# Gated products turned by the load in squares of 32 and by VectorE within them, in a two-layer adaLN feed-forward kernel

## The chip, the cores and the metric

The kernel runs on one core of a Trainium2 chip. The metric is the device time of one execution in microseconds (us), as the median of several executions.

A core has engines that run side by side, each with its own queue of instructions: TensorE (PE, matrix products; "PEld" is its loading of weights), VectorE (DVE), ScalarE (ACT), GpSimd (POOL) and SyncE (SP, which here issues nearly all transfers). Results of PE land in PSUM, everything else lies in SBUF, both with 128 partitions.

## What is computed

```python
def _L0_ffn_ref(x, A, B, Wr):
    ...
    scores = xf @ Wr.T
    top_vals, top_idx = jax.lax.top_k(scores, TOPK)          # 16 of 64
    gates = jax.nn.softmax(top_vals, axis=-1)
    G = jnp.zeros((N, K), xf.dtype).at[jnp.arange(N)[:, None], top_idx].set(gates)
    h = jnp.einsum('nd,krd->nkr', xf, A)
    out = jnp.einsum('nkr,kdr->nd', h * G[:, :, None], B)
    return (out * SCALING).reshape(*prefix, -1)
...
x = x + _L0_ffn_ref(_L0_cond_ref(x, cond_512, ...), L0_ffn_A, L0_ffn_B, L0_ffn_Wr)
x = x + _L1_ffn_ref(_L1_cond_ref(x, cond_512, ...), L1_ffn_qweight, ..., L1_ffn_bias)
```

x is (32, 64, 1024) fp32. `_cond_ref` is a chain of four one-dimensional convolutions whose weights depend on the conditioning vector. The first feed-forward layer is a mixture of 64 experts of rank 16: 2048 rows of 1024 numbers are multiplied by A (1024 x 1024, with the router's 64 columns beside it), the products h are gated, and the gated h is multiplied by B (1024 x 1024). The second feed-forward layer is a linear map whose weights are unpacked from int4.

## The kernel before

**Tiles.** The 2048 rows are cut into 16 pairs p (two samples of 64 channels, 128 rows each). `NP` is 16, `NC` is 8 (blocks of 128 along 1024), `H` is 512, `L` is 1024.

**Products in three parts.** A product in fp32 is made of three products of split operands. An operand's upper part is cut out by DVE (`high`, line 149: two shifts), DVE or POOL subtract it from the operand to get the lower part (line 918 for activations on DVE, line 374 for weights on POOL), ACT copies the upper part (lines 922 and 375) and scales the lower part of activations (line 926), and a third operand is the difference of both (line 934 for activations on POOL, line 382 for weights on DVE). In names, `thh`, `tlh` and `tdh` are upper, lower and difference of a pair's h; `hh` is the cut before the copy; `wb0` to `wb7` are B's eight row blocks with all three parts, and `wbh` the cut of one half of a block. `product` (line 954) runs first the upper and lower parts into one PSUM bank (Q), for each half of the 1024 columns, and then the difference into another (D): 48 products of 128x512 for a pair. Pairs 0 and 1 (`WHOLE`) take undivided fp32 operands instead, 16 products.

**Stages.** The first conv chain and the product with A run pair by pair (`layer0`); the gated h of pair p is stored to memory (`hgd[p]`, line 1062). Then, from about 399 to 630 us, a loop over p (line 1411) makes the product with B (`layer0b`). For each p it emits, in this order: the turning of pair p+1's h (`turned_h`), the load of pair p+2's h (`load_h`), and the product of pair p with its joins. h has its rows on partitions and must have the 1024 contracted columns there, so `turned_h` makes eight 128x128 transposes on PE (line 1078) into two PSUM banks; for pairs 0 and 1 ACT copies each bank (line 1087), for the others the split reads the bank. A join adds the product to the residual: line 1122 for the D part, line 1123 for the Q part, both on DVE, reading PSUM. After that x1 is stored and differences of its columns, `dd`, are made and stored for the next conv chain (lines 1159 to 1174).

**B's splits.** B's eight row blocks are loaded as they are (`load_b`, line 410: five blocks beside pair 14 of `layer0`, three beside pair 15). Blocks 0 to 3 are split beside the raw product of pair 0, blocks 4 to 7 beside that of pair 1; pair 2 is the first to use all of them. Each block costs two cuts on DVE (128x512), two subtractions on POOL (128x512), two copies on ACT, and one crossing on DVE (128x1024, line 382).

**Order.** Every engine runs its queue in the order in which the program emits; the exceptions are written out (`issue_after`). Next-layer work lies between the last pairs: the ends of the conv chain (lines 465 to 586), and the first conv groups of the second layer (lines 755 to 773). Buffers come from rings: "w4" with three for hs, hg, x1 and others, "hi" with three for cuts, two for `th` and `tl`, one for `td`; PSUM has three banks "cps" for turned h and conv groups and four "fps" for the products o.

Of the kernel before, what the change touches and what calls it, by code (L numbers as in the profile page):

```python
# [8 lines left out]
F32 = mybir.dt.float32  # L9
I32 = mybir.dt.int32  # L10
# [5 lines left out]
P = 128  # L16
# [8 lines left out]
NC = L // P  # L25
H = 512
# [37 lines left out]
def adaln_ffn_kernel(ctx: ExitStack, tc: tile.TileContext, t, out: bass.AP):  # L64
    nc = tc.nc
# [4 lines left out]
    wk = ctx.enter_context(tc.tile_pool(name="wk", bufs=2))  # L70
# [8 lines left out]
    def cpst(name):  # L79
        return cps.tile([P, H], F32, tag="cps", name=name)  # L80
# [8 lines left out]
    ident = const.tile([P, P], F32, name="ident")  # L89
# [28 lines left out]
    hgd = dram.tile([NP, P, L], F32, name="hgd")  # L118
# [19 lines left out]
    def tokens(tag, name, dt=F32R):  # L138

        return tok.tile([P, NC, P], dt, tag=tag, name=name, bufs=1 if tag == "td" else 2)  # L140
# [5 lines left out]
    def high(src, name):  # L146

        v = wk.tile([P, H], I32, tag="hi", name=name, bufs=3)[:, : src.shape[1]]
        nc.vector.tensor_scalar(
            v, src.bitcast(I32), BITS, BITS, ALU.logical_shift_right, ALU.logical_shift_left  # L150
        )
        return v.bitcast(F32)
# [254 lines left out]
    def load_b(ks, into):  # L407
        for k in ks:
            r = cv[:, k * L : (k + 1) * L]
            nc.sync.dma_start(r, t["bm"][k * P : (k + 1) * P])  # L410
            into.append(r)

    def load_q():
# [500 lines left out]
    def split(ps, shape, hi, lo, name, hold=False):  # L914

        uppers[name] = high(ps, name)
        h = shape(uppers[name])
        done["lo"] = nc.vector.tensor_tensor(lo, shape(ps), h, ALU.subtract)
        if hold:
            held.append((hi, h))  # L920
        else:
            nc.scalar.copy(hi, h)

    def scaled_low(v):
        v = v.rearrange("p a b -> p (a b)")
        nc.scalar.activation(v, v, AF.Copy, scale=RADIX)  # L926

    toks = {}
# [133 lines left out]
        nc.sync.dma_start(hgd[p], hs[:, E:])  # L1062

    def load_h(p):
        hg = wk.tile([P, L], F32, tag="w4", name=f"hg{p}", bufs=3)
        nc.sync.dma_start(hg, hgd[p])
        return hg

    def turned_h(p, hg):
        whole = p in WHOLE  # L1070
        key = f"h{p}"
        th = tokens("th", f"th{key}", F32 if whole else F32R)
        toks[key] = [th] if whole else [th, tokens("tl", f"tl{key}")]
        for g in range(2):
            ps = cpst(f"ht{p}_{g}")
            for c in range(4):
                k = 4 * g + c
                nc.tensor.transpose(  # L1078
                    ps[:, c * P : (c + 1) * P], hg[:, k * P : (k + 1) * P], ident
                )  # L1080
            ks = slice(4 * g, 4 * g + 4)

            def d(v):
                return v[:, ks].rearrange("p a b -> p (a b)")

            if whole:
                nc.scalar.copy(d(th), ps)
            else:
                split(ps, lambda v: v, d(th), d(toks[key][1]), f"hh{p}_{g}")
        if not whole:  # L1090
            scaled_low(toks[key][1])

# [253 lines left out]
    for k in range(NP):  # L1346
# [5 lines left out]
        if last:  # L1352
            hg = load_h(0)
# [35 lines left out]
        if last:  # L1389
            load_b(range(5, NC), braw)  # L1390
            turned_h(0, hg)
        elif k + 1 in WHOLE:
            outer(k + 1)
# [3 lines left out]
        if k == NP - 2:  # L1397
            load_b(range(5), braw)
# [6 lines left out]
        if not last:  # L1405
            crossed(f"x0_{k + 1}")

    hg = load_h(1)
    set1 = factors(1, cv[:, : 3 * AW], cv[:, 3 * AW : O_Y + Y])
    qw = None  # L1410
    for p in range(NP):
        if p + 1 < NP:
            turned_h(p + 1, hg)
        if p + 2 < NP:
            hg = load_h(p + 2)
# [127 lines left out]
```

## Time and profile before

| | us |
|---|---|
| median of 4 runs | 897.26 (896.24 to 898.35) |
| the profiled execution | 897.98 |
| its span, first to last instruction | 895.9 |

What the page and the trace show of the stage around the change:

| group | count | ns, median | where |
|---|---|---|---|
| transposes of h, PE, line 1078 | 128 | 273 | 398.7 to 584.2 us |
| ACT copies of turned h, line 1087 | 4 | 602 | 399.5 to 400.9 |
| cut of h from PSUM, DVE, line 149 | 28 | 679 | 416.1 to 587.1 |
| subtraction of the cut, DVE, line 918 | 28 | 682 | 417.9 to 587.8 |
| difference, POOL, line 934 (one at 520.26) | | 2410 | |
| cut of B, DVE, line 149 | 16 | 782 | 386.4 to 433.8 |
| subtraction for B, POOL, line 374 | 16 | 1447 | 398.1 to 435.5 |
| crossing for B, DVE, line 382 | 8 | 2062 | 401.3 to 437.6 |
| load of h, SP queue, line 1066 | 16 | | 512 KB each |

A group's median is the time of one instruction, not what it adds: PE overlaps instructions, and a queue that waits for another engine shows the wait either as idle time before the instruction or, where the engine is held within it, as a longer instruction. The starts of two successive products on PE are the surest measure of a stage; from 519.85 to 531.64 us, one pair's transposes and 48 products take 11.79 us. First products of the pairs start at 400.63 (p=0), 415.24, 429.76, 446.08, 459.06 and 471.26 us (p=5).

### The profile page before, as it was taken

How to read it: one execution, taken by the hardware profiler on the slowest of the kernel's cores; microseconds unless marked ns; L12 is line 12 of the kernel's file. 1: busy time of each engine (PE TensorE's matmuls, PEld its weight loads, DVE VectorE, ACT ScalarE, POOL GpSimd, SP SyncE). 2: the span in 40 equal slices, each digit the busy share in tenths (PEclk: the TensorE clock that was granted, in tenths of full speed). 3: DMA queues.
4: the chain of work that ended last, by engine and by line, in shares of the span. 5: the costliest groups of instructions: out<-in, count | busy, mean ns of one | idle time of the engine just before them, and what ended most of it. 6: DMA issues, size and time to landing. Idle time of an engine off the chain costs nothing.

```text
span 895.9 us, 14914 instructions
## 1 busy us (share of the span) xinstructions
PE 865.6 (97%) x5033; PEld 775.2 (87%) x5033; DVE 721.8 (81%) x1458; ACT 352.6 (39%) x817; POOL 531.6 (59%) x747
## 2 busy tenths in 40 slices
PE   5989999999999999999999999999999999999997
PEld 4877888999999999994688888787899999999997
DVE  4474898888888888778986665669999999999996
ACT  6344443444444444333332221246333443343340
POOL 7234654666666666556572222343787888888884
PEclk9999999999999999999999999999999999999999
DMA  8521212223222221344365665555433325324321
GB/s 246 148 72 54 54 56 75 77 90 88 80 84 86 83 79 71 107 176 156 136 231 193 207 193 185 188 168 173 168 123 108 107 90 148 117 90 138 122 66 71
DMA packets 49739, 109.81 MB, mean 123 GB/s; under 512 B 13700, under 2 KB 22400, under 8 KB 49664
## 3 DMA queue, kind: packets, MB, share of 16 engines
q1 hardware_dynamic: 48704, 107.88, 38.4%
q10 hardware_dynamic: 960, 0.99, 0.4%
q8 instruction: 40, 0.66, 0.3%
q14 instruction: 35, 0.29, 0.1%
HBM read 70.97 MB, written 37.88 MB: 121 GB/s over the span
## 4 chain that ended last, share of the span: by engine, by line
PE 73%; DVE 15%; issue 4%; POOL 4%; ACT 2%; DMA 2%; ACTq 0%; DVEq 0%; SPq 0%; POOLq 0%
PE h L954 18%; PE o L954 16%; PE q L1203 11%; PE f L618 6%; PE r L874 5%; PE c L772 5%; PE r L833 3%; PE r L842 2%; PE g L595 2%; PE c L767 2%; DMA x1e<-dd 1%; DVE cv L715 1%; PE p L825 1%; PE ht L1078 1%; DVE rt L865 1%
## 5 line engine op out<-in xcount | busy, mean ns | idle before, releaser
L715 DVE TENSOR_TENSOR cv<-cv 128x257 f32<-128x257 f32 x120 | 105.1, 908 | 1.3 <-ACT cv L757 0.9
L729 POOL TENSOR_TENSOR cv<-cv 128x256 f32<-128x256 f32 x120 | 77.7, 647 | 29.4 <-DVE cv L715 16.0
L721 POOL TENSOR_TENSOR cv<-cv 128x128 f32<-128x128 f32 x100 | 39.0, 411 | 67.6 <-PE r L842 48.2
L1203 PE MATMUL q<-wq,thx 128*128 128x342 f32 x384 | 73.0, 332 | 2.6 <-ACT thx L912 2.1
L954 PE MATMUL h<-wa,tdx 128*128 128x352 f32 (+1 forms) x336 | 72.4, 351 | 0.2 <-DVE wa L382 0.2
L1203 PE MATMUL q<-wq,tlx 128*128 128x342 f32 x384 | 72.4, 330 | 0.0
L618 PE MATMUL f<-gs,iw 128*128 128x128 f32 (+1 forms) x384 | 68.8, 329 | 0.0
L618 PEld LDWEIGHTS f<-gs,iw 128*128 128x128 f32 x384 | 62.5, 192 | 5.8
L954 PE MATMUL h<-wa,thx 128*128 128x352 f32 (+1 forms) x336 | 64.7, 333 | 0.0
L1203 PEld LDWEIGHTS q<-wq,thx 128*128 128x128 f32 x384 | 60.3, 189 | 4.6 <-ACT thx L912 3.2
L769 ACT ACTIVATE yt<-c,be,al 128x257 f32<-128x257 f32 x56 | 31.7, 567 | 81.1 <-PE c L767 81.0
L874 PE MATMUL r<-cv 128*128 128x128 f32 x480 | 63.4, 274 | 0.0
L1203 PEld LDWEIGHTS q<-wq,tlx 128*128 128x128 f32 x384 | 61.9, 189 | 0.8
L954 PE MATMUL h<-wa,tlx 128*128 128x352 f32 (+1 forms) x336 | 62.4, 327 | 0.0
L954 PE MATMUL o<-wb,thh 128*128 128x512 f32 x224 | 59.9, 401 | 1.5 <-ACT wb L375 1.5
L934 POOL TENSOR_TENSOR tdx<-thx,tlx 128x1024 fp32r<-128x1024 f32 x14 | 34.7, 2478 | 44.4 <-ACT tlx L926 36.2
L1122 DVE SCALAR_TENSOR_TENSOR cv<-o,cv 128x512 f32<-128x512 f32 x26 | 18.0, 691 | 51.8 <-PE o L954 51.8
L954 PEld LDWEIGHTS h<-wa,tdx 128*128 128x128 f32 x336 | 57.1, 188 | 2.4 <-DVE wa L382 0.5
L954 PE MATMUL o<-wb,tlh 128*128 128x512 f32 x224 | 58.5, 398 | 0.0
L874 PEld LDWEIGHTS r<-cv 128*128 128x128 f32 x480 | 58.4, 191 | 0.0
L633 ACT COPY cv<-f 128x256 f32<-128x256 f32 x64 | 24.0, 375 | 85.3 <-PE f L618 45.8
L641 POOL TENSOR_TENSOR cv<-cv 128x256 f32<-128x256 f32 x60 | 48.9, 815 | 12.2 <-ACT cv L636 12.2
(312 smaller groups left out, 2273.5 us busy)
## 6 DMA issues: line engine op xcount, KB each, us to landing
cv<-in_x_dram SPq DMA_DIRECT2D x60, 256.0 KB
cv<-x1e SPq DMA_DIRECT2D x64, 192.5 KB
x1e<-dd SPq DMA_DIRECT2D x16, 514.0 KB
hgd<-hs SPq DMA_DIRECT2D x16, 512.0 KB
hg<-hgd SPq DMA_DIRECT2D x16, 512.0 KB
x1d<-x SPq DMA_DIRECT2D x16, 512.0 KB
xb<-x1d SPq DMA_DIRECT2D x16, 512.0 KB
out_dram<-o SPq DMA_DIRECT2D x15, 512.0 KB
```

Source lines behind the costliest of these rows:

```text
L618: done["f"] = nc.tensor.matmul(pv[:, n : n + 2 - k], iw[:, e].rearrange("p a b -> p (a b)"), v, start=(m == 0), stop=(m == len(steps) - 1) ...
L641: nc.gpsimd.tensor_tensor(f[:, 4 * P : 6 * P].rearrange("p (a b) -> p a b", b=P), v[:, :, 0], v[:, :, 1], ALU.add,)
L715: nc.vector.tensor_tensor(d[:, k], yo[:, k : k + HQ], yb, ALU.subtract)
L721: nc.gpsimd.tensor_tensor(y[:, YB + k * P : YB + (k + 1) * P], y[:, 2 * k : 2 * k + 2 * P - 1 : 2], y[:, 1 : 2 * P : 2], ALU.subtract,)
L729: nc.gpsimd.tensor_tensor(e[:, :, k], d[:, :, 2 * k : 2 * k + HQ - 2 : 2], d[:, :, 1 : HQ - 1 : 2], ALU.subtract,)
L769: nc.scalar.activation(yt, mid, AF.Identity, bias=be0[:, n : n + 1], scale=a)
L772: done["c"] = nc.tensor.matmul(ps, w[:, q], xe[:, o : o + w_], start=True, stop=True)
L833: nc.tensor.matmul(ps[:, (2 + j) * P : (3 + j) * P], d[:, j, 1 : HQ - 1 : 2], w(6 + j), start=True, stop=True,)
L874: done["r"] = nc.tensor.matmul(ps[:, j * P : (j + 1) * P], y[:, YE + (2 * q + k) * P : YE + (2 * q + k + 1) * P], w(q + 2 * k), start=True ...
L934: done["td"] = nc.gpsimd.tensor_tensor(*(v.rearrange("p a b -> p (a b)") for v in (td, *toks[key])), ALU.subtract)
L954: nc.tensor.matmul(banks[l == 2], toks[key][l][:, order(k)], w[:, cols], start=(k == first and l != 1), stop=(k == last and l in (2, min(n ...
L1203: nc.tensor.matmul(ps, half[:, k], wq[at(k)][:, c * QC : (c + 1) * QC], start=(k == 0 and j == 0), stop=(k == NC - 1 and j == 1),)
```

## The change

The 128 transposes on PE go. A 128x128 transpose is a transpose of a 4 by 4 grid of squares of 32, and of each square within. The grid is now turned by the load: `load_h` makes four transfers, each to 32 partitions, with pieces of 256 numbers; quarter b of h's columns goes to partitions 32b to 32b+31, and quarter a of the rows lies beside it along the free axis. The squares are turned by a VectorE transpose, which turns every square of 32 by 32 by itself, two instructions of 128x512 for each pair. With this, block c of the turned h has column 256 b + 32 c + i on partition 32 b + i, and not column 128 c + partition, so `load_b` brings B's rows in the same order, by four transfers of 32 rows for each block. For pairs 0 and 1 the VectorE transpose writes the product's operand itself, and the four ACT copies go. For the others it writes a new SBUF tile, `ht`, from the ring "hi", and the split reads that tile instead of a PSUM bank.

```diff
     def load_b(ks, into):
         for k in ks:
             r = cv[:, k * L : (k + 1) * L]
-            nc.sync.dma_start(r, t["bm"][k * P : (k + 1) * P])
+            rows_of_b = t["bm"].rearrange("(b c i) d -> b c i d", b=4, c=NC)
+            for b in range(4):
+                nc.sync.dma_start(r[32 * b : 32 * b + 32], rows_of_b[b, k])
             into.append(r)
...
     def load_h(p):
+
         hg = wk.tile([P, L], F32, tag="w4", name=f"hg{p}", bufs=3)
-        nc.sync.dma_start(hg, hgd[p])
+        src = hgd[p].rearrange("(a j) (b x) -> b j a x", a=4, b=4)
+        for b in range(4):
+            nc.sync.dma_start(hg[32 * b : 32 * b + 32].rearrange("j (a x) -> j a x", a=4), src[b])
         return hg
...
         for g in range(2):
-            ps = cpst(f"ht{p}_{g}")
-            for c in range(4):
-                k = 4 * g + c
-                nc.tensor.transpose(
-                    ps[:, c * P : (c + 1) * P], hg[:, k * P : (k + 1) * P], ident
-                )
             ks = slice(4 * g, 4 * g + 4)
...
             if whole:
-                nc.scalar.copy(d(th), ps)
+                v = d(th)
             else:
-                split(ps, lambda v: v, d(th), d(toks[key][1]), f"hh{p}_{g}")
+                v = wk.tile([P, H], I32, tag="hi", name=f"ht{p}_{g}", bufs=3).bitcast(F32)
+            nc.vector.transpose(
+                v.rearrange("p (c a j) -> p a c j", c=4, a=4),
+                hg.rearrange("p (a c i) -> p a c i", a=4, c=NC)[:, :, ks],
+            )
+            if not whole:
+                split(v, lambda v: v, d(th), d(toks[key][1]), f"hh{p}_{g}")
         if not whole:
             scaled_low(toks[key][1])
```

The emission order of `turned_h`, `load_h` and `layer0b` in the loop stays. In the program as it is built, though, operations can stand elsewhere in an engine's queue than before, since some are placed by when their operands come free: on DVE the transposes of pair 1 stand behind the crossing of wb3, those of pair 2 ahead of the cuts of wb4, the copy of line 311 ahead of the second cut of wb4; in the later pairs the joins of line 1123 stand behind the second subtraction of the next pair. On SP the load of pair p+2's h stands behind the stores of an earlier pair's x1, and loads of B and of the first pairs' h stand behind the stores of h of pairs 14 and 15.

## The prediction

> **What bounds the kernel now.** The totals by engine first: TensorE (PE) is busy for 97% of the span, and the chain that ended last lies 73% on PE and 15% on VectorE (DVE). Line 1078, the transposes that the change removes, is 1% of that chain.
>
> ```profile
> PE 865.6 (97%) x5033; PEld 775.2 (87%) x5033; DVE 721.8 (81%) x1458; ACT 352.6 (39%) x817; POOL 531.6 (59%) x747
> PE 73%; DVE 15%; issue 4%; POOL 4%; ACT 2%; DMA 2%; ACTq 0%; DVEq 0%; SPq 0%; POOLq 0%
> ```
>
> Shares are averages, so next the busy time in stretches of the only stage that is touched (about 380 to 590 us). Columns: stretch and its length, busy us (instructions) of PE, PEld, DVE, ACT, POOL, then granted clock, DMA share, GB/s.
>
> ```profile
> 517.00:529.00 12.00, 12.00 (x59) 10.01 (x58) 7.09 (x10) 2.72 (x5) 2.81 (x4) 1.00 0.65 205
> ...
> 400.00:420.00 20.00, 20.00 (x58) 9.54 (x57) 16.45 (x19) 5.89 (x13) 12.14 (x11) 1.00 0.35 131
> 420.00:440.00 20.00, 18.49 (x59) 11.18 (x58) 17.66 (x16) 9.11 (x21) 15.55 (x22) 0.91 0.43 131
> 440.00:460.00 20.00, 20.00 (x108) 17.16 (x107) 17.80 (x29) 7.61 (x16) 12.80 (x19) 1.00 0.64 221
> ```
>
> The stage has two regimes. From about 470 PE is never idle and DVE rests 4.9 us of 12. Before 460 DVE is 82 to 89% busy, POOL 61 to 78%, and PE itself stops (18.49 of 20, clock 0.91). There DVE and POOL split B's eight row blocks for the products, in one in-order chain. The third view, the order of time on PE, shows that stop: product o2 waits for the copies of wb6 and wb7.
>
> ```profile
> 414.36 1.04 PE L1078 MATMUL ht<-ident,hg 128*128 128x128 f32 x8
> 415.24 13.90 PE L954 MATMUL o<-cv,thh 128*128 128x512 f32 x32
> 428.97 1.04 PE L1078 MATMUL ht<-ident,hg 128*128 128x128 f32 x8
> 429.76 1.64 PE L954 MATMUL o<-wb,thh 128*128 128x512 f32 x6
> 432.00 0.50 PE L954 MATMUL o<-wb,thh 128*128 128x512 f32 x1 [0.59 <-ACT wb L375]
> 433.41 0.50 PE L954 MATMUL o<-wb,thh 128*128 128x512 f32 x1 [0.91 <-ACT wb L375]
> ```
>
> **What is removed.** 128 transposes. Between the start of a group of eight and the next product lie 1.92 us (p=0 and 1 together, 398.70), 0.87 (414.36), and 0.79 to 0.83 for the thirteen after (the last is followed by another wait). The sum 1.92 + 0.87 + 13 × 0.81 = 13.3 us is all that PE can gain. Four ACT copies (line 1087, 602 ns) go as well; ACT is busy for 5.89 of 20 us, so that is worth nothing.
>
> **What is added on DVE.** 32 block transposes of 128x512 fp32, two for each p. The trace has none. The lower bound is the fastest 128x512 row from SBUF to SBUF, the upper the slowest with a scattered write:
>
> ```profile
> L434 DVE TENSOR_SCALAR nib<-qw x16: 414/421/961, 607.0 to 623.8; 128x512 int32<-128x512 int32 x16
> L1165 DVE TENSOR_TENSOR dd<-x x16: 671/677/1025, 416.7 to 628.2; 128x512 f32<-128x512 f32 x16
> L1123 DVE SCALAR_TENSOR_TENSOR x<-o,cv x26: 1054/1088/1105, 445.8 to 601.4; 128x512 f32<-128x512 f32 x26
> L149 DVE TENSOR_SCALAR hh<-ht x28: 672/679/691, 416.1 to 587.1; 128x512 int32<-128x512 int32 x28
> ```
>
> (ns min/median/max.) I take 0.68: the transpose reads and writes runs of 32 words, nearer to line 1165 than to line 1123's strided write. The 28 `high` operations (hh) now read SBUF instead of PSUM, so they may fall from 0.68 to 0.42: 0.26 less each. The net for a split p is 2 × 0.68 − 2 × 0.26 = +0.84 us of DVE.
>
> **The shared access.** Splits of h now take both inputs from SBUF, as does this row, whose twin at 562.56 took 0.23 us:
>
> ```profile
> 555.63 2.39 POOL L934 TENSOR_TENSOR tdh<-thh,tlh 128x1024 fp32r<-128x1024 f32 x1
> ...
> 555.70 2.40 DVE L481 TENSOR_TENSOR cv<-xg,styp 128x72 f32<-128x72 f32 x1 [0.29 <-POOL xg L1174]
> ```
>
> It ended with the POOL operation beside it. B's splits show the same: line 149's wbh takes 405 ns at best and 2204 at worst. So an hh or a subtraction that meets POOL can wait up to 2.4 us; before, from PSUM, their 28 stayed within 672 to 693 ns. [...]
>
> **Early products (p=0 to 4).** The DVE order matters here, and the built program gives it.
> - o1: th1's transposes stand behind wb3's crossing (line 382, ended 414.39). One gives 414.39 + 0.68 = 415.07 against the 415.24 of before. o0 ends 1.7 earlier, and PE then idles: gain 0.2, called 0.
> - o2: ahead of wbh6 DVE gets four transposes (th1, ht2: 2.72), loses 2 × 0.26, gets line 311's copy (1.25 at 432.63, formerly behind wbh7's first half), and loses a join (1.07, moved behind): +2.4. The subtractions beside POOL's wb splits (1.27 each) add 0 to 2.6. I take 3.5 in all: weights 6 and 7 come at 435.5 and 436.9 rather than 432.0 and 433.4. The group that is gone at 428.97 only makes the idle time longer. The wait of before halved the clock (granted 0.50 at 435 to 437); a longer one may cost 0 to 1.7 more, I take 0.8. Less the 0.83 of the group at 445.25, o3 starts +3.5 (bounds +0.7 to +6).
> - o3, o4: with DVE at 17.80 of 20, +0.84 and a lock wait (0 to 2.4) come on the path for each, less 0.8: 0 to +2.4, I take 1 each. o5 starts at +5.5 (bounds +0.7 to +8; all waits at their worst together would be too much).
>
> **Steady products (o5 to o13, eight periods).** A period is 11.78 us: 48 matmuls at 0.229 and 0.79 of transposes (starts 519.85, 531.64). DVE needs 7.09 + 0.84 = 7.9, with one wait behind tdh 10.3, of 11.0: it fits. But the order puts the second subtraction behind line 1122 of the product's very end: 0.69 + 0.68 + ACT's scaling 1.06 (line 926) + about 0.4 of hand-overs = 2.8 us, when PE has twelve matmuls, 2.75 us, to do first. So 0.1 to 0.2 is given back, and 0.55 to 0.79 gained: eight times −0.55 = −4.4 (bounds −6.3 to 0; at 1.09 a transpose DVE needs 8.8 + 2.4, over 11.0).
>
> **Tail (p=13 to 15).** Two groups go, −1.6. Two waits that stood around them, 0.30 for line 520 and 0.76 for line 465, lose that cover, and the order puts the rest of that chain (re, rt, g, f) ahead of o14; the next layer's first conv group waits for an operation that now stands behind four joins (2 × 0.69 + 2 × 1.09 = 3.5 us, with some 9 matmuls, 2.1 us, as cover). So −1.6 + 1.06 + 0.6 + 1.4 = about +1.4 (0 to +3).
>
> **Transfers.** B's eight loads become 32 and hg's sixteen become 64, each over 32 partitions. An issue takes some 0.33 us of the SP queue (line 1066), so a p adds 3 × 0.33 = 1.0 us of SP, whose five issues take 0.33 + 0.33 + 0.43 + 0.53 + 0.94 = 2.6 of 11.8 us now. hg(p+2) now stands behind x_p's stores, but it is used an iteration later (about 10 us): nothing, covered by that slack; without it, a load's 524 KB at that stretch's 205 GB/s, 2.6 us, would come each period. At the start twelve B loads, half of hg0 and all of hg1 stand behind the stores of h (391.13 and 405.25); o0 needs B by 400, so 0 to +2, taken as 0. [...]
>
> **Sum.** 0 + 5.5 − 4.4 + 1.4 = +2.5 us: 897.98 (span 895.9 and 2.1 around it) becomes 900.5 for a profiled execution. The median of the runs is 0.7 lower, 897.26, so I forecast 900 for it.
>
> **Rivals.**
> [...]
> - *A draw*: early losses of 4 paid by steady gains of 5 and a tail near +1: 897.
> [...]
> - *Loads land late*, so that a transpose waits: 2 us for each of some six products, +2.5 + 12: 912. Against: DMA share 0.65, slack of 10 us.
>
> **Numbers.** Forecast (slower by 0.2 to 0.7%) 0.36, kept 0.32, draw 0.16, DVE bound 0.12, late loads 0.04. What can be told from no change is 0.2%, 1.8 us. Faster 0.32, same 0.16, slower 0.52. The range leaves out the best of "kept" (−13.3 would be 884) and late loads: 888 to 909; the forecast's own is 897 to 905.
>
> **What would show it.** Block transposes near 0.68 us; hh near 0.42 with a tail of long ones; o1 at about 415; o2's waits for wb6 and wb7 at 434 to 438; o5 at 474 to 478 (before 471.26); periods of 11.2; DVE near 8 to 10 of 11. The forecast is wrong if o5 starts before 472, if a period is 11.7 or more, or if hg's landing is what a transpose waits for.

## The result, and the profile after

| | before | after |
|---|---|---|
| median | 896.95 us (56 runs, 895.86 to 899.13) | 899.67 us (36 runs, 897.22 to 902.25) |
| ratio to before | | 1.0025, 95% interval 1.0019 to 1.0031 |
| profiled execution | 897.98, span 895.9 | 897.30, span 895.2 |

The change costs 0.25%: 2.2 us by the ratio, 2.7 by the medians. The profiled execution of after is one of its quick ones, even below that of before; so a second execution of the same kernel was profiled as well ("again", 899.67 us, on the median), and both are used below.

The totals by engine and the chain that ended last, of after:

```profile
PE 855.9 (96%) x4905; PEld 763.3 (85%) x4905; DVE 742.4 (83%) x1490; ACT 349.8 (39%) x813; POOL 538.8 (60%) x747
PE 26%; DVE 6%; issue 1%; POOL 0%; ACT 0%; DVEq 0%; ACTq 0%
```

PE has 128 instructions and 9.7 us less to do, DVE 20.6 us more. The chain is of no use here: its first piece lies at 598 us, at the end of the stage, where before's was followed through the stage; its shares can't be set against those of before. The stretches (same columns as before: length, busy us of PE, PEld, DVE, ACT, POOL, granted clock, DMA share, GB/s) say more:

```profile
400.00:420.00 20.00, 17.61 (x42) 7.67 (x41) 17.64 (x21) 3.57 (x8) 10.89 (x9) 1.00 0.51 133
420.00:440.00 20.00, 16.26 (x50) 9.80 (x49) 12.31 (x15) 9.32 (x20) 16.14 (x21) 0.91 0.60 162
440.00:460.00 20.00, 18.02 (x79) 14.65 (x78) 19.69 (x30) 4.32 (x10) 10.46 (x15) 0.91 0.67 205
517.00:529.00 12.00, 12.00 (x54) 9.75 (x54) 10.21 (x14) 3.25 (x6) 3.23 (x4) 1.00 0.77 224
```

Steady products keep PE full, with DVE at 10.21 of 12 us instead of 7.09: the added work fits there. In the three early stretches PE now loses 2.39, 3.74 and 1.98 us of 20 each. In the second of them DVE, the engine that was given work, is *less* busy than before (12.31, before 17.66): it waits. The order of time on PE shows where PE stops:

```profile
413.77 13.97 PE L956 MATMUL o<-cv,thh 128*128 128x512 f32 x32 [2.39 <-DVE thh L1089]
427.18 1.96 PE L956 MATMUL o<-wb,thh 128*128 128x512 f32 x6
432.88 2.54 PE L956 MATMUL o<-wb,thh 128*128 128x512 f32 x5 [3.74 <-ACT wb L375]
...
442.53 5.50 PE L956 MATMUL o<-wb,tdh 128*128 128x512 f32 x16 [1.99 <-DVE x L1128]
...
448.68 2.07 PE L956 MATMUL o<-wb,thh 128*128 128x512 f32 x8
```

o1 waits for its block transposes, o2 for weight 6, and o2's D part for a join of pair 1 (line 1128 is before's 1123). Executions start differently (in before's the granted clock is 0.50 from 20.82 us, for 3.41 us; in after's it is 1.00 up to 432 us), so starts of first products are compared from the first product with A on. us, "next" being the first linear product of the second layer:

| | before | after | again | pe04 | pe24 | psum_ht | tail_o | best2 |
|---|---|---|---|---|---|---|---|---|
| o2 | 385.35 | 383.91 | 385.52 | 386.02 | 385.75 | 385.42 | 383.92 | 386.02 |
| o3 | 401.66 | 405.42 | 405.41 | 403.02 | 402.25 | 404.08 | 403.84 | 403.04 |
| o5 | 426.84 | 430.36 | 432.18 | 426.61 | 426.21 | 431.20 | 430.33 | 426.85 |
| o12 | 511.59 | 509.91 | 511.72 | 505.14 | 504.71 | 508.55 | 509.91 | 505.35 |
| next | 580.53 | 581.21 | 584.20 | 576.36 | 577.05 | 579.59 | 579.96 | 574.73 |
| end | 851.48 | 851.98 | 855.16 | 847.40 | 848.37 | 850.33 | 852.36 | 845.86 |

Read by differences: up to o5 after loses 3.5 us (again 5.3), from o5 to o12 it gains 5.2 in both, from o12 to next it loses 2.4 (again 3.5). The gain is real, and it is paid back on both sides of it.

### The profile page after: what moved, and what is told of

Read it like the earlier page. It is cut to its first block, busy times and chain, and to the rows that moved or that the text cites. A ratio compares the mean times of both kernels' runs of the same rounds, so it can differ in the third digit from the quotient of the medians.

```text
span 895.2 us, 14768 instructions
## 1 busy us (share of the span) xinstructions
PE 855.9 (96%) x4905; PEld 763.3 (85%) x4905; DVE 742.4 (83%) x1490; ACT 349.8 (39%) x813; POOL 538.8 (60%) x747
## 5 line engine op out<-in xcount | busy, mean ns | idle before, releaser
L731 POOL TENSOR_TENSOR cv<-cv 128x256 f32<-128x256 f32 x120 | 77.9, 650 | 27.6 <-DVE cv L717 22.9
L1179 POOL COPY xg<-x 128x8 f32<-128x8 f32 x32 | 10.6, 335 | 79.8 <-DVE x L1128 73.8
L643 POOL TENSOR_TENSOR cv<-cv 128x256 f32<-128x256 f32 x60 | 50.5, 842 | 13.1 <-ACT cv L638 13.1
L956 PE MATMUL o<-wb,tdh 128*128 128x512 f32 x224 | 56.2, 401 | 2.0 <-DVE x L1128 2.0
```

The lines of the kernel that those rows point to most:

```text
L643: nc.gpsimd.tensor_tensor(f[:, 4 * P : 6 * P].rearrange("p (a b) -> p a b", b=P), v[:, :, 0], v[:, :, 1], ALU.add,)
L731: nc.gpsimd.tensor_tensor(e[:, :, k], d[:, :, 2 * k : 2 * k + HQ - 2 : 2], d[:, :, 1 : HQ - 1 : 2], ALU.subtract,)
L956: nc.tensor.matmul(banks[l == 2], toks[key][l][:, order(k)], w[:, cols], start=(k == first and l != 1), stop=(k == last and l in (2, min(n ...
L1179: nc.gpsimd.tensor_copy(xg[:, p, s].rearrange("p (j f) -> p j f", f=4), v[:, js])
```

## The experiments

Each was timed beside before on the same chip; intervals are 95%.

| run | what it is | median | ratio to before |
|---|---|---|---|
| pe04 | pairs 0 to 4 by PE | 893.68 | 0.9962 (0.9949 to 0.9975) |
| pe512 | pairs 5 to 12 by PE | 904.39 | 1.0081 (1.0068 to 1.0095) |
| pe012 | pairs 0 to 12 by PE | 897.93 | 1.0002 (0.9992 to 1.0012) |
| no_turn | block transposes left out | 896.34 | 0.9984 (0.9970 to 0.9998) |
| early | queue order held as before | 898.97 | 1.0014 (1.0001 to 1.0027) |
| tail_o | conv work of the tail held behind o14 | 898.87 | 1.0016 (1.0007 to 1.0024) |
| pe01 | pairs 0 and 1 by PE | 896.20 | 0.9987 (0.9976 to 0.9998) |
| pe24 | pairs 2 to 4 by PE | 893.73 | 0.9959 (0.9945 to 0.9973) |
| psum_ht | turned h in PSUM | 895.24 | 0.9973 (0.9960 to 0.9986) |
| best | pe04 and tail_o | 893.29 | 0.9959 (0.9946 to 0.9971) |
| best2 | best, re and rt moved too | 891.54 | 0.9937 (0.9917 to 0.9957) |

**Which stage pays: pe04, pe512, pe012.** Some pairs are turned by PE again. B's rows stay in the new order, so the store of those pairs' h puts its columns into that order.

```diff
+    BY_DVE = range(5, 16)          # pe512: (0,1,2,3,4,13,14,15); pe012: range(13, 16)
...
+    def store_h(p, hs):
+        if p in BY_DVE:
+            nc.sync.dma_start(hgd[p], hs[:, E:])
+            return
+        dst = hgd[p].rearrange("r (c b i) -> r b c i", b=4, c=NC)
+        src = hs[:, E:].rearrange("r (b c i) -> r b c i", b=4, c=NC)
+        for b in range(4):
+            nc.sync.dma_start(dst[:, b], src[:, b])
...
     def load_h(p):
         hg = wk.tile([P, L], F32, tag="w4", name=f"hg{p}", bufs=3)
+        if p not in BY_DVE:
+            nc.sync.dma_start(hg, hgd[p])
+            return hg
...
+            if p not in BY_DVE:
+                ps = cpst(f"ht{p}_{g}")
+                for c in range(4):
+                    k = 4 * g + c
+                    nc.tensor.transpose(ps[:, c * P : (c + 1) * P], hg[:, k * P : (k + 1) * P], ident)
...
+                continue
```

> The changed kernel, but the h of pairs 0 to 4 is turned by TensorE again, from a plain load; their store brings the columns into the order of B's rows (pieces of 128 bytes, long before use). B's loads stay in 32 quarters, pairs 5 to 15 stay with the block transposes. Theory 1 (the loss lies in VectorE's work between 398 and 475 us, while B is split): the first product of pair 5 comes within 1 us of where it was before the change, the steady pairs keep their gain of 0.8 each, the tail its loss of some 2, and the time is 897 - 6 + 2 = 893 to 894.5. Rival (the quarter loads of B, or the order at the end, are what costs): 898 to 900.

> The changed kernel, but the h of pairs 5 to 12 is turned by TensorE again, in the manner of the first run; pairs 0 to 4 and 13 to 15 keep the block transposes. Theory 1 (steady pairs gain 0.75 to 0.8 each): 899.7 + 8 x 0.77 = 905 to 906.5. Rival (the steady pairs gain little in most executions, and the profiled one was lucky): 900 to 902.

> Only pairs 13, 14 and 15 keep the block transposes; pairs 0 to 12 are turned by TensorE as before the change, B still comes in quarters. Theory 1 (the tail loses some 2 us net of its three groups, by the chain of small products put ahead of pair 14 and by the convolution group that waits behind joins): 898.5 to 899.5. Rival (the tail gains its three groups, 0.8 each, and the loss seen at the end is only handed on from earlier): 894.5 to 896.5.

pe04 against after: (0.9962 − 1.0025) × 897 = −5.7 us, and o5 comes at 426.61, where before has it (426.84): the early loss hangs on the first five pairs, and B's quarter loads, which pe04 keeps, cost nothing that shows at o5. pe512 is 5.0 us worse than after: that is the steady gain, taken away (its median lies a little under the range expected). pe012 ends beside before, between its two ranges; its stage from o12 on takes 69.69 us, against 68.94 of before. So the tail alone gives no gain, and in this one profile a small loss.

**Is it DVE's time? no_turn.** The transposes go, everything else stays.

```diff
+            v = hg[:, g * H : (g + 1) * H]
             if whole:
-                v = d(th)
+                nc.vector.tensor_copy(d(th), v)
             else:
-                v = wk.tile([P, H], I32, tag="hi", name=f"ht{p}_{g}", bufs=3).bitcast(F32)
-            nc.vector.transpose(
-                v.rearrange("p (c a j) -> p a c j", c=4, a=4),
-                hg.rearrange("p (a c i) -> p a c i", a=4, c=NC)[:, :, ks],
-            )
-            if not whole:
                 split(v, lambda v: v, d(th), d(toks[key][1]), f"hh{p}_{g}")
```

> The changed kernel with the 32 block transposes left out: the split reads the loaded h as it is (pairs 0 and 1: a plain copy on VectorE in the transpose's place), so the squares are not turned. Loads, cuts and subtractions from SBUF stay. Theory 1 (VectorE's added time in the early stage is what costs): pair 5 starts 3 to 5 us earlier than in the changed kernel, and the time is 894.5 to 897. Rival (the waits of cuts and subtractions from SBUF for GpSimd, and the new order, cost it; the transposes' own 0.7 us are hidden in waits): 898.5 to 900.

Without its transposes (the four of the whole pairs become copies) the kernel is 3.7 us quicker than after: (0.9984 − 1.0025) × 897. But its o3 comes at 405.58, not earlier than in after (405.42) and again (405.41); only from o3 to o5 it is quicker, 23.9 us against 24.9 in after and 26.8 in again. Its o5 is 2.6 later than before. The time lies in the range of theory 1, the start of pair 5 does not: it is 0.9 us earlier than in after and 2.7 than in again, not 3 to 5. The order of time on DVE in that run:

```profile
420.15 0.95 DVE L149 TENSOR_SCALAR wbh<-cv 128x512 int32<-128x512 int32 x2 [1.73 <-ACT thh L924]
425.48 1.47 DVE L149 TENSOR_SCALAR wbh<-cv 128x512 int32<-128x512 int32 x1 [4.38 <-POOL wb L374]
```

DVE stands idle for 6.1 us in front of B's cuts, with no block transpose in its queue. A part of the loss is the transposes' time all the same. In no_turn o1 takes 15.67 us, as it does in again (13.97 in after); so these two can be compared, PE in no_turn and then in again:

```profile
432.69 0.50 PE L956 MATMUL o<-wb,thh 128*128 128x512 f32 x1 [2.57 <-ACT wb L375]
434.44 0.79 PE L956 MATMUL o<-wb,thh 128*128 128x512 f32 x1 [1.25 <-ACT wb L375]
```

```profile
433.72 1.44 PE L956 MATMUL o<-wb,thh 128*128 128x512 f32 x4 [3.75 <-ACT wb L375]
435.48 0.80 PE L956 MATMUL o<-wb,thh 128*128 128x512 f32 x1 [0.32 <-ACT wb L375]
```

Counted from the first product with A (42.71 and 42.50 us), weights 6 and 7 come 1.2 us earlier in no_turn; it loses that again within o2, where the next two groups of eight matmuls take 3.61 and 2.95 us (from 435.03), in again 2.86 for the first eight (from 436.07) and 1.97 for eight from 439.91. So some 1.2 of the 3.8 us up to o3 can be put down to the transposes; the rest lies in waits between the queues and the slower matmuls behind them.

**Is it the new order of the queues? early.** after has the same sort of waits. On ACT, then DVE, then POOL:

```profile
421.77 0.47 ACTq L199 DMA_DIRECT2D cv<-in_cw_dram  x1
422.28 0.62 ACT L924 CAST thh<-hh 128x512 fp32r<-128x512 f32 x1 [3.17 <-PE o L956]
```

```profile
422.63 0.18 DVE L311 COPY cv<-cv 128x32 f32<-128x32 f32 x1 [1.92 <-PE o L956]
...
424.47 0.43 DVE L149 TENSOR_SCALAR wbh<-cv 128x512 int32<-128x512 int32 x1 [1.00 <-ACT wb L375]
...
430.61 1.23 DVE L382 SCALAR_TENSOR_TENSOR wb<-wb 128x1024 fp32r<-128x1024 f32 x1 [3.50 <-POOL dd L1169]
```

```profile
425.99 3.37 POOL L936 TENSOR_TENSOR tdh<-thh,tlh 128x1024 fp32r<-128x1024 f32 x1
429.32 1.26 POOL L374 TENSOR_TENSOR wb<-cv,wbh 128x512 fp32r<-128x512 f32 x1
```

The copy of pair 2's second half stands on ACT behind the issue of a parameter load (line 199), which overwrites raw B and so waits for o1; in before that issue came after these copies. Line 311's copy, moved ahead of B's cuts on DVE, waits for o1 likewise (1.92). ACT's late copy holds a buffer of the ring "hi", DVE stalls, and POOL takes the difference `tdh` ahead of B's subtraction, for which DVE then waits 3.50 us (the row names the short fill of line 1169 that POOL does right behind it). Together DVE idles 6.4 us between 420 and 431. The run early holds line 311 behind the crossings, that load behind B's copies, `tdh` of pair 2 behind B's subtractions, and pair 1's first join ahead of the cuts of blocks 6 and 7:

```diff
+        with nullcontext() if i == 0 else tc.issue_after(done["crossed"].ins):
+            nc.vector.tensor_copy(be[:, 3], bib(3))
...
+        if p == 1:
+            split_weights(braw, L, range(4, 6), wb, "wb")
+            with tc.issue_after(done["join1_0"].ins):
+                split_weights(braw, L, range(6, 8), wb, "wb")
...
+            with tc.issue_after(done["low_wb7"].ins) if p == 1 else nullcontext():
+                crossed(f"h{p + 1}")
...
+                with tc.issue_after(done["up_wb7"].ins) if p == 1 else nullcontext():
+                    next(set1, None)
```

> The changed kernel with all its block transposes, but four things of pairs 1 and 2 are held to an order like that of before: the copy of line 311 behind B's crossings, pair 2's difference on GpSimd behind B's subtractions, pair 1's first join ahead of the cuts of wb6 and wb7, and the first parameter loads on ScalarE's queue behind B's copies. VectorE has the same work. Theory 2 (formed after the run without transposes: pair 5 came only 0.9 us earlier there, so the loss is waits that the new order brought in, not VectorE's time): pair 5 starts 2.5 to 3.5 us earlier than in the changed kernel and the time is 896 to 897.5. Theory 1 (VectorE's added time): no more than 1 us of gain, 899 to 900.

It missed: 898.97, o5 at 432.89. The order of time on PE shows why:

```profile
438.20 0.50 PE L959 MATMUL o<-wb,thh 128*128 128x512 f32 x1 [1.47 <-ACT wb L378]
...
442.05 3.94 PE L959 MATMUL o<-wb,tdh 128*128 128x512 f32 x16 [1.52 <-POOL tdh L939]
451.44 0.82 PE L269 MATMUL dps<-cv 128*128 128x32 f32 x3 [5.45 <-DVE cv L239]
```

The wait of 3.74 for weight 6 is gone, and in its place stand weight 7 (1.47), the difference that was put behind (1.52) and then 5.45 us. Even so o2's D part begins 12.1 us after o2, against 15.4 in after and again and 11.1 in before: with all block transposes still on DVE, an order near that of before gives back 3.2 of the 4.3 us lost there. Some 1.6 of the 3.2 is the clock (an estimate: in after 3.12 us of PE's work there fall into the stretch from 432.59 to 436.00 us at a granted clock of 0.50, half of which is 1.6; in early two groups of eight matmuls there take 2.01 and 2.00 us), and 0.8 goes the other way, since the small product sps (line 232) stands within o2 here. The 5.45 us this run brought in itself: dps, a small product for the next conv's parameters (line 269), stands ahead of o3 on PE here, and behind o3 in after (459.66 us, without a wait). ACT's copies of o3's upper part are done at 446.48; o3 begins at 453.88. So the new order of the queues carries a good part of the loss up to o2's D part, and the miss at o5 does not speak against that. Which of the four moves counts is not told apart.

**Which relief cures it: pe01, pe24, psum_ht.** pe01 and pe24 are pe04 with other pairs. psum_ht leaves all transposes on DVE, but writes them where PE wrote before, which frees the ring "hi" and lets the split read PSUM again.

```diff
             else:
-                v = wk.tile([P, H], I32, tag="hi", name=f"ht{p}_{g}", bufs=3).bitcast(F32)
+                v = cpst(f"ht{p}_{g}")
```

> The changed kernel, but pairs 0 and 1 alone are turned by TensorE and copied by ScalarE as before; pairs 2 to 15 keep the block transposes. If the early loss is the late turning of pair 1 (2.4 us of idle TensorE before o1, and the half clock that can follow): 896 to 897.5. If it is the split pairs 2 to 4 (cuts and subtractions from SBUF, four transposes among B's cuts): 898.5 to 900.

> The changed kernel, but pairs 2, 3 and 4 alone are turned by TensorE and split from PSUM; pairs 0, 1 and 5 to 15 keep the block transposes. The counterpart of the run before: if the early loss is the late turning of pair 1, 898.5 to 900; if it is the split pairs, 894.5 to 896.5.

> The changed kernel, but the block transposes of pairs 2 to 15 write a PSUM bank, which the cut and the subtraction read, as before the change. Cuts go back from 0.43 to 0.68 us (0.5 more per pair on VectorE), the waits for GpSimd at the cuts and subtractions go, and the ring hi has its three buffers to itself. If waits for GpSimd or for the ring make the early loss: pair 5 starts 1.5 to 3 us earlier, 897 to 898.5. If neither: 0.5 x 4 pairs more early, 900 to 902.

Against after they gain 3.4, 5.9 and 4.7 us; pe04, which is the first two together, gains 5.7, not 9.3. By time each of pe01 and pe24 speaks for its own theory, so the two together decide for neither. In pe24, o1 still waits for DVE, but o2's stops are back to the size of before (PE in order of time):

```profile
413.48 1.10 PE L957 MATMUL o<-cv,thh 128*128 128x512 f32 x2 [2.37 <-DVE thh L1114]
...
431.14 0.50 PE L957 MATMUL o<-wb,thh 128*128 128x512 f32 x1 [0.55 <-ACT wb L376]
432.89 0.50 PE L957 MATMUL o<-wb,thh 128*128 128x512 f32 x1 [1.25 <-ACT wb L376]
```

So it is enough to give the turning of pairs 2 to 4 back to PE, and their splits back to PSUM, while B is still being split; to take only the block transposes off DVE, as no_turn does, is not. pe24's profile flatters o5 (426.21): before's granted clock is 0.50 from 433.83 us, for 3.41 us, and eight matmuls there (433.75) take 3.53 us, in pe24 (433.22) 2.17. Half of the 3.41, 1.7 us, is an estimate of what that is worth. Its median, 893.73, rests on eight runs and lies below both ranges. psum_ht, at 895.24 below both of its ranges too, does not work that way: its o5 comes at 431.20, a microsecond before that of again, and the rest of its gain lies later (o5 to o12 77.4 us against 79.5, o12 to next 71.0 against 72.5). It changes ring and operand place at once, so the two are not told apart; a longer ring alone was not tried.

**Two executions of after: again.** The same kernel, a second execution.

> The changed kernel once more, for a second profile. Its times lie in groups that go with the granted clock (897.5 at 0.993, 899.8 at 0.991). If the groups differ by one more stretch of half clock in the stage where B is split, this profile shows 0.991 with such a stretch, or 0.993 without; each costs about 1.7 us.

o1 in this execution (order of time on PE), and stretches of 3.41 us around it, first of again and then of after:

```profile
412.91 15.67 PE L956 MATMUL o<-cv,thh 128*128 128x512 f32 x32 [2.36 <-DVE thh L1089]
```

```profile
410.60:414.01 3.41, 1.10 (x3) 0.65 (x4) 3.06 (x5) 0.00 (x0) 0.28 (x1) 1.00 0.29 108
414.01:417.42 3.41, 3.41 (x5) 1.37 (x5) 3.41 (x6) 0.00 (x0) 0.71 (x2) 0.50 0.23 44
```

```profile
408.70:412.11 3.41, 2.68 (x7) 0.89 (x5) 2.25 (x2) 0.36 (x1) 3.04 (x2) 1.00 1.00 225
412.11:415.52 3.41, 1.75 (x4) 0.87 (x5) 3.38 (x6) 0.00 (x0) 0.00 (x0) 1.00 0.21 73
415.52:418.93 3.41, 3.41 (x9) 1.52 (x8) 3.41 (x6) 0.63 (x2) 0.70 (x2) 1.00 0.31 64
```

The same wait before o1 (2.36 and 2.39 us) is followed by half clock in one execution (granted 0.50 from 414.01 us in again) and not in the other (1.00 in after), and o1 takes 15.67 instead of 13.97 us. The stretches are laid so that their borders meet those of each execution's half clock (414.01 in again, 432.59 in after). In again the wait then falls into one stretch, which leaves PE 1.10 of 3.41 us; in after it is cut in two, 0.73 and 1.66 us. o2 starts 1.6 us later in again, and DVE, whose copy of line 311 waits for o1, falls behind by as much. At o3 the two are level all the same: in after a stretch at a granted clock of 0.50 (442.83 to 446.24) falls on o2's D part, which takes 5.50 us (above); in again it takes 3.88 us:

```profile
443.38 3.88 PE L956 MATMUL o<-wb,tdh 128*128 128x512 f32 x16 [1.50 <-DVE x L1128]
```

DVE stays behind, and at o5 again is 1.8 us later. The stage in which B is split thus shows two stretches at a clock of 0.50 in either execution (from 414.01 and 434.49 us in again, 432.59 and 442.83 in after), not one more in again, though again's mean clock is 0.991 against 0.993. Where again's further half clock lies is not shown here. From the first product with A to the end again takes 3.2 us more: 1.8 up to o5, 1.2 from o12 to next, 0.2 after that. That the 1.8 us come from o1's clock alone is not shown.

**The tail, and a version that beats both: tail_o, best, best2.** PE in order of time, in after:

```profile
578.10 0.84 PE L549 MATMUL re<-cv,cw 128*128 128x48 f32 x6 [0.74 <-DVE cv L522]
579.63 0.29 PE L558 MATMUL rt<-ident,cv 128*48 128x128 f32 x1 [0.69 <-POOL cv L467]
580.27 1.13 PE L597 MATMUL g<-r,tw 128*128 128x256 f32 x4 [0.35 <-ACT cv L560]
582.23 0.70 PE L620 MATMUL f<-gs,iw 128*128 128x256 f32 x2 [0.82 <-ACT gs L609]
...
598.62 0.70 PE L774 MATMUL c<-cv 128*128 128x257 f32 x2 [1.43 <-DVE cv L775]
599.75 1.16 PE L774 MATMUL c<-cv 128*128 128x256 f32 x2 [0.43 <-DVE cv L775]
```

Four links of one dependent chain stand in front of o14, each with a wait, and the conv group c waits for DVE, where the joins come first. tail_o holds g, f and c behind the first half of pair 14's D part. best joins that to pe04. best2 also moves re and rt behind the first half of pair 14's product.

```diff
             begin(NP)
-            compose(NP)
-            conv(NP, 0)
-            weights(NP)
+            with tc.issue_after(done[f"o{p}_0"].ins):
+                compose(NP)
+                conv(NP, 0)
+                weights(NP)
...
+        if p == LAST + 2:                              # best2 only
+            with tc.issue_after(done[f"q{p}"].ins):
+                run(set_ends)
...
-        if p in (LAST, LAST + 1):
+        if p == LAST:
             next(set_ends)
...
-        if p == LAST + 1:
-            run(set_ends)
```

> The changed kernel, but the next layer's small products (lines 595, 618, and its first convolution groups) are queued on TensorE behind the first difference part of pair 14, where they stood before the change; all else stays. Theory (the tail's loss is that order): from pair 12 to the end of the stage 1.5 to 2.5 us less, 897.2 to 898.3. Rival (the tail's waits are VectorE's, and only move): 899.2 to 900.

> The kernel with pairs 0 to 4 turned by TensorE, and the order of the run before on TensorE at pair 14. If both parts add: 893.7 - 2 = 891 to 892.5. If the tail's order is worth nothing: 893 to 894.

> The kernel best (pairs 0 to 4 turned by TensorE, small products of the next layer held behind pair 14's first difference part), and the last steps of the conv ends (re and rt, lines 547 and 556) are moved from between pairs 13 and 14 to behind the first half of pair 14's product. In best they stood in TensorE's queue before pair 14 with waits of 0.74, 0.68 and 0.55 us and a stretch of half clock after them. If those waits are what is left of the tail's loss: 2 to 3.5 us less than best, 889.5 to 891.5. If they are only handed on: 892.5 to 893.5.

tail_o brings o12 to next from 71.30 to 70.05 us, best2 to 69.38, near before's 68.94. In time tail_o lies between its two ranges, 0.8 us below after and within the intervals, so its gain is not shown by time. best gained little over pe04 (medians 893.29 and 893.68), as expected if the tail's order is worth nothing, and its profile shows re and rt still waiting, and o14 slow behind them, its first eight matmuls taking 3.66 us, where they take 2.07 in before and 2.19 in after:

```profile
576.06 0.29 PE L559 MATMUL rt<-ident,cv 128*48 128x128 f32 x1 [0.68 <-POOL cv L468]
576.90 3.66 PE L957 MATMUL o<-wb,thh 128*128 128x512 f32 x8 [0.55 <-DVE cv L1152]
```

best2, with block transposes for pairs 5 to 15 only, is quicker than before and after: 0.9937 (0.9917 to 0.9957), 891.54 us. Its gain over best, 1.75 us by the medians, is less than the 2 to 3.5 expected, and the intervals overlap. What it leaves is mainly one wait, again on PE, with eight slow matmuls behind it (3.60 us):

```profile
574.05 3.60 PE L957 MATMUL o<-wb,thh 128*128 128x512 f32 x8 [1.86 <-DVE cv L1152]
...
584.84 0.77 PE L550 MATMUL re<-cv,cw 128*128 128x48 f32 x6
```

## Why the prediction was right, point by point

The sum was +2.5 us, and the medians differ by 2.7. Its three terms have the right signs; their sizes are off and partly cancel, so that the sum comes this close is luck in part. One reading was too smooth: before's PE is not free of idle time from 470 us on. It is so in the steady pairs; at 569.04 us it waits 1.18 us for POOL, and 0.30 and 0.76 around the last transposes.

- *Prices.* Of after, from views of single lines and tiles (ns min/median/max), and then two of psum_ht:

```profile
L1089 DVE STREAM_TRANSPOSE ht<-hg x28: 668/703/712, 414.1 to 585.2; 128x512 f32<-128x512 f32 x28
L149 DVE TENSOR_SCALAR hh<-ht x28: 408/426/1122, 414.8 to 586.6; 128x512 int32<-128x512 int32 x28
L920 DVE TENSOR_TENSOR tlh<-ht,hh x28: 648/679/1529, 417.6 to 587.0; 128x512 fp32r<-128x512 f32 x28
```

```profile
L149 DVE TENSOR_SCALAR hh<-ht x28: 656/667/692, 414.6 to 584.6; 128x512 int32<-128x512 int32 x28
L920 DVE TENSOR_TENSOR tlh<-ht,hh x28: 662/673/691, 416.9 to 585.8; 128x512 fp32r<-128x512 f32 x28
```

  The block transpose was put at 0.68 and takes 0.70; hh was put at 0.42 and takes 0.43. From SBUF hh is quicker in the median (426 ns) and has a tail, up to 1122; from PSUM it is slower (667) and has none (692 at most), and neither has the subtraction (1529 at most from SBUF, 691 from PSUM). The block transposes, 712 ns at most, have none in after. The price was small, though: means of 450 and 705 against medians of 426 and 679 ns, 1.4 us over 56 operations.
- *o1, called 0.* The start (370.5 us after the first product with A, 370.8 in before) and the wait (2.4 by the prediction's figures, 2.39 measured) were as predicted. What the step left out is the clock: in again half clock (granted 0.50 from 414.01 us) follows the wait that "called 0" accepted, and o1 takes 15.67 us, 1.70 more than in after. Half clock was priced at o2 alone.
- *o2, +3.5 at o3.* Measured +3.8 in both executions, by two ways. Weight 6, put at 3.5 us late, is 3.6 late in again, with o1's half clock in it, and 2.0 in after. Weight 7 adds no wait in after and 0.32 in again, and then the D part waits 1.99 (again: 1.50) for the join of pair 1; in after a stretch at a clock of 0.50 falls on that part as well, and it takes 5.50 us against 3.88 in again. Moving that join was counted as −1.07 for weight 6; the step didn't ask who waits for the join, and its sign was wrong. The stall on ACT behind line 199's issue was not seen at all: the order of the queues was told for DVE and SP, and not for ACT. And the working summed DVE's time ahead of weight 6; without the block transposes, in no_turn, weight 6 comes 1.2 us earlier than in again and o3 no earlier, while early, which keeps them, gives back 3.2 us before o2's D part, the clock included.
- *o3 and o4, +1 each.* From o3 to o5 after takes 24.94 us and before 25.18: −0.2 instead of +2; again takes 26.77, +1.6. So o5 is +3.5 in one execution and +5.3 in the other, against +5.5. The working counts a "lock wait" of 0 to 2.4 us for each; no run shows a lock. What after shows there is an hh of 1122 ns (at 457.15 us) and a subtraction of 1529 (458.30), beside POOL's line 252, 1.5 us over their medians together.
- *Steady, −0.55 a period.* From o5 to o12, seven periods, −5.2: −0.74 each. The plain ones measure 10.92 to 11.00 us against 11.79, and 10.88 in pe04, so no more than 0.1 is given back; the step took 0.1 to 0.2 and then chose the low end of its gain. DVE, put at 8 to 10 of 11, is at 10.21 of 12; its largest extra is not an hh but line 1170, which falls beside `tdh` (DVE, then POOL, order of time):

```profile
523.87 2.09 DVE L1170 TENSOR_TENSOR dd<-x 128x512 f32<-128x512 f32 x1 [0.20 <-DVE x L1128]
```

```profile
523.02 2.40 POOL L936 TENSOR_TENSOR tdh<-thh,tlh 128x1024 fp32r<-128x1024 f32 x1
```

  It ends within 0.6 us of POOL's operation, and PE does not wait for it.
- *Tail, +1.4.* The two mechanisms named are those of the profile: re, rt, g and f ahead of o14, and c behind the joins. The term was too small: +2.4 and +3.5 from o12 on. It counted the waits of re and rt (1.06 became 1.43) and took 0.6 for the others, which are 0.35 + 0.82 in after, and again had no price for the clock (0.50 from 599.85 us in after, for 3.41 us).
- *Transfers, nothing.* Right, though not cheap on SP: in the steady pairs the four quarter loads of h take 2.4 to 3.6 us of its queue where the step put 4 × 0.33. No transpose waits for hg. How a quarter load fares by itself no run here shows.

The rivals: that the removed time is kept ("kept", 0.32) needed an early chain that does not lengthen, and weight 6 was 2.0 and 3.6 us late; pe04 and pe24, which keep the gain by turning early pairs on PE, come to 893.7. That DVE becomes the bound in all periods ("DVE bound", 0.12) fell with the periods of 11.0, "loads late" with the waits, which are for ACT, DVE and POOL.

What stays open is which of the waits between 420 and 443 us starts the early loss. Three reliefs give it back wholly or in part, they don't add up, and holding four of the moves back gained 3.2 us up to o2's D part but only 1 us in the time, within the intervals, as it also set another product ahead of o3; that the queues of DVE, ACT and POOL stop each other there is shown, a single first cause is not.

## What to carry to other kernels

Work that is moved from a full engine to one with idle time should be judged stage by stage: here it gains 0.8 us a pair where the receiving engine only has its own work, and loses it all where that engine feeds a chain of weights and the order of the queues changes with it, so moving it for some pairs only beats both kernels. A new operand takes a buffer ring and an order in every queue, those of the untouched engines included; look for a transfer issue or a copy that waits for a product and has got ahead of something urgent. An idle time of PE need not be over with its end: here 2.36 us of it before o1 in again was followed by 3.41 us at a granted clock of 0.50, and o1 took 1.70 us more than in after.

## What the hardware showed unexpectedly

In before and after, between 20 and 890 us, the granted clock is 0.50 in stretches of 3.41 us and 1.00 elsewhere, and in each execution their starts lie whole steps of that length apart: 20.82 and 433.83 in before (121 steps of 3.413 us), 432.59, 442.83 and 599.85 in after (3 and 46), 414.01 and 434.49 in again (6). With the execution cut into these steps, from 17 us on, half clock came behind steps in which PE idled for 2.02 and 1.51 us (before, from 17.41 and 430.42), 3.41, 1.98 and 1.86 (after, from 429.18, 439.42 and 596.43), 2.31 and 2.64 (again, from 410.60 and 431.08) and 3.29 (early, from 445.87). The longest idle times with full clock behind them are 1.66, 1.43 and 1.42 us in after (from 412.11, 579.37 and 463.31) and 1.19 and 1.18 in before (from 51.54 and 566.95). So in these executions a step need not be idle throughout: 1.51 of 3.41 us came ahead of half clock, while 1.66 came ahead of full. Of the steps already at half clock, one in which PE idled for 2.16 us (early, from 449.28) was followed by another, and one with 0.32 (again, from 434.49) and one with 0.29 (after, from 432.59) by full clock. So 2.4 us of idle time before o1 was followed by 1.70 us more for that product in again, where it lay in one step, and by nothing in after, where it lay in two. Of after's 36 runs, nine have a mean clock of 0.993 and a median of 897.53, nineteen 0.991 and 899.81. Which wait parts them is not shown: the two profiled executions have two stretches at half clock each where B is split.
